# Attention followed by two quantized convolutions: products with v in half steps, and what moves with them

## The chip, the cores and the metric

The kernel runs on one core of a Trainium2 chip. The metric is the time of one execution on the device in microseconds (us); lower is better. A profiled execution gives its own time, and a span from its first to its last instruction.

## What is computed

An input x of 4 images, 128 channels, 64 x 64 positions goes through a group norm, an attention over the 4096 positions with four heads of 32 channels, a projection and a residual sum. The result goes through two 3 x 3 convolutions with weights quantized to 3 bits, each followed by a batch norm; the first has a relu, the second adds its input and then has a relu. The reference, cut:

```python
x_norm = _group_norm(x, norm_w, norm_b)
qkv = jnp.einsum('oc,bchw->bohw', qkv_w, x_norm) + qkv_b[None, :, None, None]
...
attn = jnp.einsum('bhid,bhjd->bhij', q, k) * scale
attn = jax.nn.softmax(attn, axis=-1)
out = jnp.einsum('bhij,bhjd->bhid', attn, v)
...
out = jnp.einsum('oc,bchw->bohw', proj_w, out) + proj_b[None, :, None, None]
x = x + out
...
residual = x
out = conv3x3_decomposed(x, lsq_quantize(w1, alpha1))
out = jax.nn.relu(batchnorm(out, gamma1, beta1))
out = conv3x3_decomposed(out, lsq_quantize(w2, alpha2))
out = batchnorm(out, gamma2, beta2)
out = jax.nn.relu(out + residual)
```

`lsq_quantize` divides the weights by a step, clips, rounds and multiplies back.

## The kernel before

**Blocks and steps.** The attention is cut into 32 blocks, eight blocks of 512 queries (`qb`) for each of four images (`b`), and each block into 32 steps (`kt`) of 128 keys. A step has two score pairs and the products with v. `scores` computes one pair, that is two heads: eight TensorE matmuls of 512 columns into a PSUM tile `s` of two banks (three such tiles rotate), and one ScalarE exponential of 128 x 1024 (L437) into half of a tile `p`. The `p` tiles come from `ppool`, which has eight buffers. `weights` does the products of a step: for each of the four heads a matmul of 128 x 32 weights from v with 512 columns of `p`, which the profile shows as two records, all added into one bank `acc` over the block (L448). The four heads use four column tiles of the array side by side; four matmul records that run together are called a group below. The scores use two row tiles.

**Sums.** The softmax's denominator is the sum of all `p` of a block. VectorE adds 26 of the 32 tiles (L458, L460); the steps in `MOVED` are added by DMAs that POOL issues (L453, L455), and `merge` (L481) joins the two. The matmuls of `total` (L477) sum over partitions.

**The order on TensorE** is written out by hand: three pairs, one step of products, three pairs, two steps of products, and so on. Scores run ahead of products. Side work is put at places given by steps: `schedule(n, before)` returns a list of (step, function), and after each step of products `side` runs what is due. `slots` are the steps whose number in the whole run is divisible by 3, which are those done singly; the matmuls of side work go there. Side work of a block is: the end of the block before (`sums`, `spread`, `invert`, `gather`, `weigh`, `project`, `store`), the projections to q, k and v of the next image's chunks of 512 positions (`project_parts`, in `visit`, with the copy of the result one step later: for k and q L344 on ScalarE and L345 on VectorE, for v L364 on VectorE), group norm statistics, and loads. For image 0 the chunks are projected in blocks 0 and 1 from two `p` tiles that hold x (`xh`).

**Quantization.** `quant_tasks` yields pieces: for each of the two convolutions nine scalar operations, and three times three taps, each with a load (L172) and thirteen VectorE operations (L174 to L189) into the resident tiles `wq[0]` and `wq[1]`. The pieces are taken up six to a block, in blocks of the last image from its second on.

**Convolutions.** Images are cut into bands of 16 rows. A band is loaded (`load_band`, issued by SP), split into two parts of fewer bits (`split_band`, VectorE, L562 and L563), and each half band takes 18 matmuls of 512 columns (L752). The first two bands are loaded and split in the last attention block; the third is loaded after `sums_at_once` and split after the last `store`. The later ones follow in `first(m)`. After that `att.close()` gives the attention's memory to the convolution's tiles (`mid`). At the end each of 16 pieces is scaled and added (L912, VectorE), goes through a relu (L913, ScalarE) and leaves by a DMA issued by SP (L914).

Queues work in order: an instruction that waits holds up what stands behind it on its engine, DMA issues on SP, POOL and ACT among them.

Of the kernel before, what the change touches and what calls it, by code (L numbers as in the profile page):

```python
# [16 lines left out]
F32 = mybir.dt.float32  # L17
# [5 lines left out]
P = 128  # L23
GROUP = 16
HEADS = 4
D = 32
# [52 lines left out]
def _fast_body(ctx, tc, x, norm_w, norm_b, qkv_wt, qkv_b, proj_wt, proj_b,  # L79
# [57 lines left out]
    wq = [const.tile([P, TAPS, P], F32R, name=f"wq{i}") for i in range(2)]  # L137
# [3 lines left out]
    def quant_tasks(pool):  # L141

        tasks = []
        for i, (w, alpha) in enumerate(((w1, alpha1), (w2, alpha2))):
# [20 lines left out]
            for c in range(3):  # L165


                def taps(i=i, c=c, w=w, t=t):
                    tk, tq = (pool.tile([P, 2, FB], F32, name=f"t{n}{i}{c}", tag=n) for n in "kq")
                    wr, q0, qh, ql = (u[:, e, : 3 * P].rearrange("p (t o) -> p t o", o=P)  # L170
                                      for u in (tk, tq) for e in range(2))
# [17 lines left out]
                    nc.vector.tensor_scalar(wq[i][:, 3 * c : 3 * c + 3, :], q0, ROUND, None,  # L189
                                            ALU.subtract)  # L190
# [9 lines left out]
    dram = ctx.enter_context(tc.tile_pool(name="dram", bufs=1, space=bass.MemoryType.DRAM))  # L200
# [11 lines left out]
    ppool = att.enter_context(tc.tile_pool(name="ppool", bufs=8))  # L212
# [228 lines left out]
    def weights(step):  # L441
# [3 lines left out]
        if kt == 0:  # L445
            acc[n] = psa.tile([P, FB], F32, name=f"acc{n}", tag="a")
        for h in range(HEADS):
            nc.tensor.matmul(acc[n][h * D : (h + 1) * D, :], v[:, kt % KB, h * D : (h + 1) * D],  # L448
                             pt[:, h, :], start=(kt == 0), stop=(kt == NK - 1))
# [172 lines left out]
    def schedule(n, before):  # L622
        b, qb = blocks[n]
        todo = []
        slots = [kt for kt in range(NK - 1) if (n * NK + kt) % 3 == 0]
        two = b + 1 < B and qb in (2, 3)
        full = two or n == 1

        def add(kt, f):
            todo.append((kt, f))  # L630

        def visit(kts, first, second, evacuate=None):
            add(kts[0], first)
            add(kts[-1], second)
            if evacuate:
                add(kts[-1] + 1, evacuate)

        if before:
            add(1, before["merge"])
            kts = slots[3:4] if full else slots[3:5]  # L640
            visit(kts, lambda: before["sums"](0), lambda: before["sums"](1))
            kt = kts[-1]
            add(kt + 1, before["spread"])
            add(kt + 3, before["invert"])
            add(kt + 4, before["gather"])
            add(kt + 6, before["residual"])
            add(slots[9] - 2, before["weigh"])
            add(slots[9], before["project"])
            add(slots[9] + 1, before["store"])
        if n + 1 < len(blocks):  # L650
            add(22 if n == 0 else 14, lambda: load_q(*blocks[n + 1]))
        if n == 0:
            for kt, what, j in ((0, "k", 4), (3, "k", 5), (6, "v", 4), (9, "k", 6), (12, "v", 5),
                                (15, "k", 7), (18, "q", 1), (21, "v", 6), (24, "v", 7)):
                visit((kt,), *first_chunk(j, what, False))
                if what == "k":
                    add(kt + 2, lambda j=j: load_k(0, j))
        if n == 1:
            for i, j in zip((0, 1, 2, 4, 5, 6), range(2, NB)):
                visit(slots[i : i + 1], *first_chunk(j, "q", False))  # L660
        if b + 1 < B:
            if qb == 1:
# [6 lines left out]
                for i in (0, 1):  # L669
                    add(slots[7 + i], late[b][1 + 2 * i])  # L670
                    add(slots[7 + i] + 1, late[b][2 + 2 * i])
            if qb == 2:
                add(slots[0], late[b][5])
                add(slots[0] + 1, late[b][6])
                add(slots[0] + 1, late[b][7])
                add(slots[0] + 2, late[b][8])
            chunks = {1: (), 2: (0, 1), 3: (2, 3), 4: (4,), 5: (5,), 6: (6,), 7: (7,)}
            for i, j in enumerate(chunks.get(qb, ())):
                p = project_parts(b + 1, j, lambda j=j: xin[b + 1, j])
                if not two:  # L680
                    places = dict(k=slots[0:2], q=slots[5:7], v=slots[7:9])
# [692 lines left out]
```

## Time and profile before

| what | us |
|---|---|
| runs before: median of 3 (lowest, highest) | 2571.59 (2570.69, 2572.87) |
| profiled execution, its own time | 2571.87 |
| its span | 2570.1 |
| attention, from the first pair to the last product | 25 to 2256 |
| first convolution, to its last matmul | 2256 to 2398 |
| second convolution, to its last matmul | 2402 to 2540 |
| scaling and output | 2540 to 2570 |

The granted TensorE clock is 0.994 of the full one on average. In lines of the timeline the columns are: start, length, engine, source line, operation, tiles and shapes, number of instructions merged into the line, and in brackets how long the engine idled before and what ended that. The length of a matmul line reaches past the start of the next one, since matmuls are pipelined and their ends are modelled; the distance between starts is what TensorE takes. In a table of windows the columns are the stretch, its length, the busy time (and number) of PE, PEld, DVE, ACT and POOL, then the clock, the share of the 16 DMA engines, and GB/s. In a group of the page: busy time, mean ns of one, and the idle time before with its releaser.

### The profile page before, as it was taken

How to read it: one execution, taken by the hardware profiler on the slowest of the kernel's cores; microseconds unless marked ns; L12 is line 12 of the kernel's file. 1: busy time of each engine (PE TensorE's matmuls, PEld its weight loads, DVE VectorE, ACT ScalarE, POOL GpSimd, SP SyncE). 2: the span in 40 equal slices, each digit the busy share in tenths (PEclk: the TensorE clock that was granted, in tenths of full speed). 3: DMA queues.
4: the chain of work that ended last, by engine and by line, in shares of the span. 5: the costliest groups of instructions: out<-in, count | busy, mean ns of one | idle time of the engine just before them, and what ended most of it. 6: DMA issues, size and time to landing. Idle time of an engine off the chain costs nothing.

```text
span 2570.1 us, 48634 instructions
## 1 busy us (share of the span) xinstructions
PE 2526.5 (98%) x20504; PEld 1231.7 (48%) x20504; DVE 2139.0 (83%) x1401; ACT 2083.9 (81%) x2278; POOL 280.3 (11%) x459
## 2 busy tenths in 40 slices
PE   9999999999999999999999999999999999999995
PEld 5444444444444444444444444444444444467774
DVE  6898888888988889889988888888999998854345
ACT  5888899998989899998988899998889899911224
POOL 2111111111011111110011111110000001000000
PEclk9999999999999999999999999999999999999997
DMA  6777666788667767787766666986755756635004
GB/s 193 186 189 177 173 157 156 167 195 192 164 144 183 173 156 166 161 214 175 165 171 158 164 158 151 205 202 141 160 115 131 164 125 141 147 79 162 1 1 165
DMA packets 147562, 400.06 MB, mean 156 GB/s; under 512 B 59256, under 2 KB 60024, under 8 KB 118792
## 3 DMA queue, kind: packets, MB, share of 16 engines
q0 software_dynamic: 45792, 280.33, 48.4%
q1 hardware_dynamic: 100824, 115.10, 16.9%
q8 instruction: 163, 2.67, 0.4%
q10 hardware_dynamic: 720, 1.44, 0.2%
q14 instruction: 63, 0.52, 0.1%
HBM read 105.32 MB, written 55.83 MB: 63 GB/s over the span
## 4 chain that ended last, share of the span: by engine, by line
PE 82%; DVE 9%; DMA 4%; issue 3%; ACT 1%; SPq 0%; POOL 0%; DVEq 0%; POOLq 0%; ACTq 0%
PE s L435 36%; PE acc L448 32%; PE c L752 9%; DVE r L460 6%; DMA rm<-p 4%; PE l L477 1%; PE pk L310 1%; PE pq L310 1%; PE po L310 1%; PE pv L310 1%; ACT p L437 1%; DVE res L912 1%; PE c_last L752 0%; DMA xh<-in_x_dram 0%; DVE r L458 0%
## 5 line engine op out<-in xcount | busy, mean ns | idle before, releaser
L437 ACT ACTIVATE p<-s 128x1024 f32<-128x1024 f32 x2048 | 1940.3, 1032 | 229.3 <-PE s L435 153.8
L460 DVE TENSOR_TENSOR r<-r,p 128x2048 f32<-128x2048 f32 x768 | 1758.4, 2290 | 93.8 <-ACT p L437 45.1
L435 PE MATMUL s<-q,k 64*128 64x512 f32 x8192 | 1160.5, 412 | 3.1 <-ACT p L437 2.5
L448 PE MATMUL acc<-p,v 128*32 128x512 f32 x8192 | 1021.9, 601 | 0.5 <-DVE v L364 0.5
L435 PEld LDWEIGHTS s<-q,k 64*128 64x128 f32 x8192 | 709.1, 185 | 632.5 <-issue 296.1
L448 PEld LDWEIGHTS acc<-p,v 128*32 128x32 f32 x8192 | 197.8, 108 | 452.9 <-issue 446.1
L455 POOL DMA_DIRECT2D rm<-p x160 | 138.5, 866 | 946.4 <-ACT p L437 770.1
L817 ACT COPY cv<-c 128x512 f32<-128x512 f32 x60 | 35.3, 588 | 201.9 <-DVE st L816 201.9
L752 PE MATMUL c<-hi,wq 128*128 128x512 f32 x540 | 139.2, 402 | 2.8 <-DVE hi L562 1.6
L752 PE MATMUL c<-lo,wq 128*128 128x512 f32 x540 | 138.6, 401 | 0.0
L816 DVE BATCH_NORM_STATS2 st<-c 128x6 f32<-128x512 f32 x60 | 41.9, 699 | 104.3 <-PE c L752 84.1
L752 PEld LDWEIGHTS c<-hi,wq 128*128 128x128 f32 x540 | 101.2, 188 | 32.5 <-DVE hi L562 2.5
L752 PEld LDWEIGHTS c<-lo,wq 128*128 128x128 f32 x540 | 101.6, 188 | 27.1
L458 DVE TENSOR_TENSOR r<-p,p 128x2048 f32<-128x2048 f32 x32 | 73.3, 2290 | 23.9 <-ACT p L437 23.8
L345 DVE SCALAR_TENSOR_TENSOR kst<-pk,b,kst 128x512 fp32r<-128x512 f32 x32 | 24.0, 750 | 72.1 <-ACT kst L344 72.1
L345 DVE SCALAR_TENSOR_TENSOR qst<-pq,b,qst 128x512 fp32r<-128x512 f32 x32 | 24.0, 750 | 41.5 <-ACT qst L344 41.3
L481 POOL DMA_DIRECT2D r<-rm x31 | 26.3, 849 | 162.0 <-PE s L435 79.8
L453 POOL DMA_DIRECT2D rm<-p x32 | 17.8, 558 | 228.6 <-ACT p L437 142.9
L349 POOL DMA_DIRECT2D qd<-qst x31 | 23.1, 747 | 177.9 <-DVE qst L345 160.8
L349 POOL DMA_DIRECT2D kd<-kst x28 | 20.7, 738 | 167.5 <-DVE kst L345 164.1
L477 PE MATMUL l<-r,ones 128*32 128x256 f32 (+1 forms) x504 | 37.9, 383 | 0.5 <-issue 0.5
L310 PE MATMUL po<-av,wp 128*32 128x512 f32 x256 | 33.4, 594 | 4.2 <-DVE av L526 4.2
(146 smaller groups left out, 722.9 us busy)
## 6 DMA issues: line engine op xcount, KB each, us to landing
rm<-p POOLq DMA_DIRECT2D x192, 1024.0 KB, 7.9
q<-qd SPq DMA_DIRECT2D x248, 128.0 KB
r<-rm POOLq DMA_DIRECT2D x31, 1024.0 KB, 7.7
x<-in_x_dram SPq DMA_DIRECT2D x80, 256.0 KB
k<-kd SPq DMA_DIRECT2D x124, 128.0 KB
qd<-qst POOLq DMA_DIRECT2D x31, 512.0 KB, 5.9
kd<-kst POOLq DMA_DIRECT2D x28, 512.0 KB, 3.7
y<-x POOLq DMA_DIRECT2D x32, 256.0 KB, 4.8
```

The lines of the kernel that those rows point to most:

```text
L310: nc.tensor.matmul(out[cs, :], w[:, cs], x, start=True, stop=True)
L345: nc.vector.scalar_tensor_tensor(lo, ps[what], bias, t[:, 0, :], ALU.add, ALU.subtract)
L349: (nc.sync if start else nc.gpsimd).dma_start(out=dst[b, j].rearrange("s p n -> p s n"), in_=t)
L435: nc.tensor.matmul(s[:, i, :], k[r, half, c0 : c0 + P], q[r, half, part, :], start=(part == 0), stop=(part == 1))
L437: nc.scalar.activation(pts[step][:, 2 * half : 2 * half + 2, :], s, AF.Exp, scale=SCALE)
L448: nc.tensor.matmul(acc[n][h * D : (h + 1) * D, :], v[:, kt % KB, h * D : (h + 1) * D], pt[:, h, :], start=(kt == 0), stop=(kt == NK - 1))
L455: nc.gpsimd.dma_start(out=msum[n], in_=pt, accum_op=ALU.add)
L458: nc.vector.tensor_tensor(rsum[n], pts[step - 1], pt, ALU.add)
L460: nc.vector.tensor_tensor(rsum[n], rsum[n], pt, ALU.add)
L477: nc.tensor.matmul(t["l"][h * D : (h + 1) * D, cs], ones, r[:, h, cs], start=first, stop=end)
L752: nc.tensor.matmul(ps.rearrange("p (r w) -> p r w", w=W), w[:, tap, :], part[:, r0 + kh : r0 + kh + RB, kw : kw + W], start=(n == 0), stop ...
L816: nc.vector.bn_stats(st[:, b * NB + c, :], ps[:, j, :])
```

## The change

Seven things are changed together.

1. **Half steps.** `weights(step, half)` does 256 of the 512 columns of a step. The order is now three pairs and three half steps throughout; before the first, six pairs are done instead of five. Only the first matmul of the first half starts the accumulation, and only the last of the second half ends it. Sums and moved tiles follow the second half.
2. **Places in half steps.** `ends` are the last half steps of each round of three, 21 in a block where `slots` had 10 or 11. Side work is put there with `at_half`; `visit` takes the index of a place and does both halves there, or on it and the next with `split`. The copy of a projection follows one half step after its second half.
3. **Image 0.** Queries 2 to 7 of image 0 are projected from x that is loaded again, so that `xh` is free after block 0. Statistics and projections of image 1 start one block later, and three blocks instead of two take two chunks each.
4. **`ppool` has nine buffers.** The room comes from `wq[1]`.
5. **Quantization.** Three pieces a block in the last image's first seven blocks; six and five in the first blocks of the second and third image. The second convolution's weights go to DRAM (`wqd`) by DMAs of POOL, are loaded again after `att.close()` by SP, and are copied to `wq[1]` by VectorE in `first(6)`.
6. **Third band.** Loaded in the last block and split ahead of `sums_at_once`.
7. **Output.** Every other piece leaves by a DMA that ScalarE issues.

The diff, cut to its core:

```diff
-    wq = [const.tile([P, TAPS, P], F32R, name=f"wq{i}") for i in range(2)]
+    wq = [const.tile([P, TAPS, P], F32R, name="wq0")]
+    wqd = dram.tile([P, TAPS, P], F32, name="wqd")
...
+                    if i == 0:
+                        nc.vector.tensor_scalar(wq[0][:, cs, :], q0, ROUND, None, ALU.subtract)
+                    else:
+                        nc.vector.tensor_scalar(ql, q0, ROUND, None, ALU.subtract)
+                        nc.gpsimd.dma_start(out=wqd[:, cs, :], in_=ql)
+                    yield
...
-    ppool = att.enter_context(tc.tile_pool(name="ppool", bufs=8))
+    ppool = att.enter_context(tc.tile_pool(name="ppool", bufs=9))
...
-    def weights(step):
+    def weights(step, half):
...
+        cs = slice(half * FB // 2, (half + 1) * FB // 2)
         for h in range(HEADS):
-            nc.tensor.matmul(acc[n][h * D : (h + 1) * D, :], v[:, kt % KB, h * D : (h + 1) * D],
-                             pt[:, h, :], start=(kt == 0), stop=(kt == NK - 1))
+            nc.tensor.matmul(acc[n][h * D : (h + 1) * D, cs], v[:, kt % KB, h * D : (h + 1) * D],
+                             pt[:, h, cs], start=(kt == 0 and half == 0),
+                             stop=(kt == NK - 1 and half == 1))
+        if half == 0:
+            return
...
-        slots = [kt for kt in range(NK - 1) if (n * NK + kt) % 3 == 0]
-        two = b + 1 < B and qb in (2, 3)
+        ends = [p for p in range(2 * NK - 2) if (2 * n * NK + p) % 3 == 2]
+        two = b + 1 < B and qb in ((3, 4, 5) if b == 0 else (2, 3))
...
+        def visit(i, first, second, evacuate=None, split=True):
+            at_half(ends[i], first)
+            e = ends[i + 1 if split else i]
+            at_half(e, second)
             if evacuate:
-                add(kts[-1] + 1, evacuate)
+                at_half(e + 1, evacuate)
+            return e
...
+                    for what, i in dict(k=1, q=10, v=13).items():
+                        visit(i, *p[what])
+                    continue
+                for what, e in (dict(k=2, q=7, v=9) if i == 0 else dict(k=11, q=13, v=15)).items():
+                    visit(e, *p[what], split=False)
...
-        if b == B - 1 and 0 < qb < NB - 1:
-            for kt in range(1, NK - 1, 5):
+        if b == B - 1 and qb < NB - 1:
+            for kt in (1, 10, 20):
                 add(kt, lambda: next(pieces, None))
+        elif 0 < b and qb == 0:
+            for kt in (1, 10, 15, 20, 25) + ((29,) if b == 1 else ()):
+                add(kt, lambda: next(pieces))
...
+            add(27, lambda: load_band(0, 2))
...
-    run_scores(2)
-    while at["step"] < steps:
-        for s, w in ((3, 1), (3, 2)):
-            run_scores(s)
-            run_weights(w)
+    run_scores(3)
+    while at["half"] < 2 * steps:
+        run_scores(3)
+        run_weights(3)
...
     conv(ready[0, 0, 0], early[0][:, 1, :], 1, wq[0])
+    split_band(*bandlist[2])
     last["sums_at_once"]()
-    load_band(*bandlist[2])
...
     last["store"]()
-    split_band(*bandlist[2])
...
+    raw_w = mid.tile([P, TAPS, P], F32, name="raw_w")
+    wq.append(mid.tile([P, TAPS, P], F32R, name="wq1"))
+    nc.sync.dma_start(out=raw_w, in_=wqd)
...
+        if m == 6:
+            nc.vector.tensor_copy(wq[1], raw_w)
...
-                nc.sync.dma_start(out=out[b].rearrange("c h w -> c (h w)")[:, cs], in_=y)
+                eng = nc.sync if j % 2 == 0 else nc.scalar
+                eng.dma_start(out=out[b].rearrange("c h w -> c (h w)")[:, cs], in_=y)
```

## The prediction

> **What bounds the kernel now.** I read the page's busy times first, then its costliest groups.
>
> ```profile
> PE 2526.5 (98%) x20504; PEld 1231.7 (48%) x20504; DVE 2139.0 (83%) x1401; ACT 2083.9 (81%) x2278; POOL 280.3 (11%) x459
> ...
> L437 ACT ACTIVATE p<-s 128x1024 f32<-128x1024 f32 x2048 | 1940.3, 1032 | 229.3 <-PE s L435 153.8
> L460 DVE TENSOR_TENSOR r<-r,p 128x2048 f32<-128x2048 f32 x768 | 1758.4, 2290 | 93.8 <-ACT p L437 45.1
> L435 PE MATMUL s<-q,k 64*128 64x512 f32 x8192 | 1160.5, 412 | 3.1 <-ACT p L437 2.5
> L448 PE MATMUL acc<-p,v 128*32 128x512 f32 x8192 | 1021.9, 601 | 0.5 <-DVE v L364 0.5
> ```
>
> TensorE looks always busy, so only stretches that are longer than they need be can be won. To find them I went through the timeline of PE for the whole attention part (25 to 2256 us) and sorted its 682 rounds, a round being three score pairs and the products with v behind them. A stretch without side work, with ACT beside it:
>
> ```profile
> 1893.47 1.66 PE L435 MATMUL s<-q,k 64*128 64x512 f32 x12
> 1894.25 5.61 ACT L437 ACTIVATE p<-s 128x1024 f32<-128x1024 f32 x6 [0.60 <-PE s L435]
> 1895.06 1.06 PE L448 MATMUL acc<-p,v 128*32 128x512 f32 x8
> 1896.06 1.84 PE L435 MATMUL s<-q,k 64*128 64x512 f32 x12
> 1897.83 1.92 PE L448 MATMUL acc<-p,v 128*32 128x512 f32 x16
> ```
>
> From start to start: three pairs 1.59 us, one step of products 1.00, three pairs again but 1.77, two steps 1.85. The second group of pairs is the stretched one, and ACT then idles 0.60 us per two rounds. A round with side work:
>
> ```profile
> 1942.24 1.67 PE L435 MATMUL s<-q,k 64*128 64x512 f32 x12
> 1943.84 1.06 PE L448 MATMUL acc<-p,v 128*32 128x512 f32 x8
> 1944.73 0.61 PE L477 MATMUL l<-r,ones 128*32 128x256 f32 x8
> 1945.27 1.67 PE L435 MATMUL s<-q,k 64*128 64x512 f32 x12
> ```
>
> This round takes 3.03 us and the pairs after it start 1.60 us ahead of their products: nothing is stretched. Over all rounds the means are: pairs 1.595; one step of products 0.996, two steps 1.854; 0.432 more for eight side matmuls of 256 columns, 0.863 for sixteen, 0.857 for eight of 512. What exceeds these is the whole reserve, 37 us: 21.9 in pairs after the 117 short rounds (2.59 us, no side work; 0.19 each), 4.3 in a few other pairs that wait up to 1.2 us, mostly for a p buffer (ACT waits on the DMA rm<-p 4.5 us in all), 8.2 in product phases, 2.7 at the start. Where the products wait, VectorE is late:
>
> ```profile
> 1908.11 2.29 DVE L460 TENSOR_TENSOR r<-r,p 128x2048 f32<-128x2048 f32 x1
> 1910.31 0.68 DVE L526 TENSOR_TENSOR av<-av,rc 128x512 f32<-128x512 f32 x1
> ...
> 1911.05 1.07 PE L310 MATMUL po<-av,wp 128*32 128x512 f32 x8 [2.45 <-DVE av L526]
> ```
>
> That block (1846.74 to 1917.20) has VectorE busy 68.4 of 70.5 us. Last, the convolution's one hole and the end:
>
> ```profile
> 2277.70 2.42 PE L752 MATMUL c<-hi,wq 128*128 128x512 f32 x9 [1.56 <-DVE hi L562]
> ...
> 2556.00:2560.00 4.00, 0.00 (x0) 0.00 (x0) 4.00 (x4) 3.85 (x4) 0.00 (x0) 0.50 1.02 407
> ```
>
> The last columns of the window are clock, DMA share and GB/s: all 16 DMA engines are full while the output leaves.
>
> **What the Trainium skill says.** "TensorE: Matmul & The Clock Gate", section "Wait — 56ns, not 53.3ns?", gives a fixed cost of about 2.5 ns per matmul beside its columns. The trace agrees: two groups of 256 columns take 432 ns, one of 512 takes 429 (0.858/2). The same page's opening table says that TensorE's queue pulls weight loads ahead of running matmuls. The trace agrees: the four loads of a group (0.13 us) lie under the group before. "TensorEngine Tiling (Array Packing)", section "Key Properties": changing the tiling mode drains the engine. It fits 0.996 - 0.858 = 0.138 us once per product phase; the number of changes stays. "Trainium Kernel Development and Optimization", section "Key Constraints": DMAs issued by SP, ACT and POOL share the same 16 engines, and issuing from several saves issue time only. The share of 1.02 with one queue agrees.
>
> **The change part by part**, against the profiled execution, 2571.87 us (span 2570.1 and 1.8 around it; 0.3 above the median of the runs).
>
> *Equal phases.* Every round becomes three pairs and three half steps: 1.595 + 0.138 + 1.294 = 3.03 us. ACT needs 2.86 for three exponentials. In the quoted stretch ACT begins 0.78 us after the pairs do and has released the third bank at 0.78 + 2.86 = 3.64; a short round wants to write it at 2.59 + 1.07 = 3.66, which, with the release taking about 0.18, gives the measured 0.17 to 0.19. A 3.03 us round wants it at 4.10, so 0.28 remains. In the trace the 141 rounds near 3.03 us are followed by pairs with no excess beyond one-off waits. All 21.9 go: **-21.9**.
>
> *Halves.* Each step has four groups of 256 columns instead of two of 512: 2048 more groups at 2.4 ns, **+5.0** (683 phases x 0.0074). Their loads (16,384 instructions added, half of them loads) hide under groups of 216 ns, as those of pv hide under 109 ns groups.
>
> *ACT's other work.* Bias copies of k and q (L344, 0.70 us busy) are queued half a step after the visit, thus behind the next round's three exponentials. Before, that was a two-step round with 0.6 us of ACT idle; now it is a 3.03 us one with 0.17. The next exponential comes about 0.36 us late against 0.28 of cover: 0.1 us. There are 59 such copies, and where the round behind one carries a side product it costs nothing; with the copies of acc and l I take half of 6 us, **+3**. Bounds: 0, and the whole 0.36 x 59 = 21.
>
> *Nine p buffers.* The DMA rm<-p holds a tile 7.9 us in the median and 14.8 at most; a ninth buffer gives a step (2.1 us) more, above the longest single wait (1.4): -3.3 of the 4.3, since other small waits may sit there (bounds 0 and -4.3). Dropping xh after block 0 frees two more in block 1.
>
> *Quantization.* Three taps cost 13 VectorE operations, 6.2 us by their rows, 37 in all. Before, six pieces per block put about 9 us into each of blocks 25 to 28; now three pieces are 3.7 us in blocks 24 to 30, and 6 to 8 in blocks 8 and 16, which have no projections. The waits of po on av (4.2 us) and the stretched pairs behind the longest (0.8) go: **-5.0**. Block 8 is followed by a block with bn_stats (8 x 0.69 us), where VectorE has little left: **+1**, bounds 0 and 4. The second weights' three stores on POOL and the single reload are 1.2 MB of 400 and cost nothing. POOL waits for ql before each store; behind it stands an rm<-p with one buffer more of slack.
>
> *Third band.* Its split moves into the 7 us in which VectorE is idle ahead of L499: -1.6. But the reload of the second weights stands on SP ahead of the fourth band's load and goes to memory that the attention's tiles held; the memset of L807, to the same region, waited until 2279.9 for VectorE. If the load waits as long, the band lands about 5 us later, near 2285, when TensorE (from 2276.1, 8.6 us on) wants it: +1, bounds 0 and +3. Together **-0.6**. The copy to wq1 (some 0.8 us of VectorE) lies in one of the 4.4 us gaps ahead of L816.
>
> *Output on two queues.* Sixteen half-megabytes at 405 GB/s are 21 us, from 2545 to 2566.3; a second queue adds no engine. ACT now issues eight of them (SP's take 0.33 us each): two activations and an issue are about 2.6 us against 2.6 for two transfers. **0**, bounds -0.8 (the one gap near 2546) and +2.
>
> Sum: -21.9 + 5.0 + 3 - 3.3 - 5.0 + 1 - 0.6 = -21.8, so 2550.1, and **2550** beside the median. Start (2.7), sums, projections, load rates and the convolutions stay. What is late next is TensorE itself: 2.02 us a step with nothing left to squeeze.
>
> **Rivals.**
> 1. *Bias copies cost their whole shift.* For it: ACT's idle time per round falls from 0.6/2 to 0.17. Against: the slack of 0.28. Time: 2550 + 18 = 2568. Chance 0.10.
> 2. *Half groups don't stream* (slower). In the product phases of 24 matmuls and 24 loads, a group takes 0.226 us instead of 0.216, because a load of 0.13 us is not always finished, or 1.8 times the product instructions don't arrive in time. 4096 groups x 0.010 = 41: 2591. It decides from 22/4096, some 5 ns a group. For it: so long a run of half groups is nowhere in the trace. Against: 16 side matmuls of 256 follow eight of 512 at 0.216, and 32 of 128 columns at 0.109. Chance 0.09.
> 3. *No residue*: no late ACT, all p waits gone, the whole 1.6 at the band: 2550 - 3 - 1 - 1 - 1 - further product waits of 3 = 2541. Chance 0.07.
> 4. Forecast: 0.74, its own range 2542 to 2561.
>
> **How the numbers follow.** About 0.2% (5 us) is what this kernel's measurement tells from no change. Faster, below 2566.4: forecast, no residue and a third of the first rival, 0.84. Within: the rest of that rival, 0.07. Slower: 0.09. The range 2540 to 2569 takes in the first rival and leaves out the slow one and the far ends, under 0.2 together.
>
> **What would show it.** Pairs at 1.60 us in nearly every round and rounds of 3.03; product phases of 1.43 with 24 matmuls; no po wait on av near 1900; the hole at 2277.70 gone or below 1.5 us; the end still at 400 GB/s. Groups of 256 above 0.22 us, or pairs above 1.65 us in the second round after bias copies, would make it wrong.

## The result, and the profile after

| | before | after |
|---|---|---|
| median of 6 runs each, us | 2573.67 | 2566.55 |
| ratio of after to before (95% interval) | | 0.9976 (0.9963 to 0.9989) |
| the profiled execution, us | 2571.87 | 2569.21 |
| its span | 2570.1 | 2567.4 |
| first pair | 25.2 | 28.5 |
| attention, first pair to the copy of the last acc | 2231.2 | 2222.9 |
| from there to the end of the span | 313.7 | 316.0 |

The kernel got faster by 0.24%, 7 us in the medians. The forecast was 21.8 us. The two profiles differ by 2.7 us only, because the profiled execution of the changed kernel began its attention 3.3 us later. That is not the change: the kernel before with one edit inside the attention (b_halves, below) begins at 28.7 us too. The start goes with TensorE's granted clock ahead of the first pair. In the profile of the kernel before the clock does not fall back there; in five of the variants below it falls to half for 3.4 us, and they begin between 26.8 and 27.6; in the changed kernel and the seven others it does so for 6.8 us, and they begin between 28.1 and 29.4. So attention and the rest are compared stage by stage here, and whole times by their medians.

The page of the changed kernel, first the busy times and then its costliest groups (busy time, mean ns of one, idle time before them and its main releaser):

```profile
PE 2515.2 (98%) x28696; PEld 1504.3 (59%) x28696; DVE 2137.1 (83%) x1402; ACT 2086.7 (81%) x2278; POOL 282.9 (11%) x462
...
L444 ACT ACTIVATE p<-s 128x1024 f32<-128x1024 f32 x2048 | 1949.6, 1032 | 216.0 <-PE s L442 161.4
L471 DVE TENSOR_TENSOR r<-r,p 128x2048 f32<-128x2048 f32 x768 | 1758.2, 2289 | 69.4 <-ACT p L444 18.7
L442 PE MATMUL s<-q,k 64*128 64x512 f32 x8192 | 1140.6, 409 | 6.7 <-ACT p L444 5.5
L456 PE MATMUL acc<-p,v 128*32 128x256 f32 x16384 | 1027.1, 383 | 1.0 <-DVE v L371 1.0
```

The scores (L442, L435 before) lost 20 us of busy time, the products (L456, L448 before) with twice the matmuls gained 5. This is what the change was made of, and it is close to the forecast. The last field of the scores' row has grown: 5.5 us in which TensorE waited for an exponential, against 2.5 before. The lines of TensorE and ScalarE in the timeline of a stretch without side work:

```profile
1930.62 1.50 PE L456 MATMUL acc<-p,v 128*32 128x256 f32 x24
1932.06 1.64 PE L442 MATMUL s<-q,k 64*128 64x512 f32 x12
1932.83 5.85 ACT L444 ACTIVATE p<-s 128x1024 f32<-128x1024 f32 x6 [0.17 <-PE s L442]
1933.63 1.50 PE L456 MATMUL acc<-p,v 128*32 128x256 f32 x24
1935.06 1.65 PE L442 MATMUL s<-q,k 64*128 64x512 f32 x12
```

From start to start: pairs 1.57 us, products 1.43, again and again. ACT idles 0.17 us per round instead of 0.60 per two. Over the whole attention, 665 of 682 rounds have pairs between 1.56 and 1.62 us, 1.595 in the median, and product phases without side work take 1.43. In the steady state the forecast (1.595 and 1.432) came out to the hundredth. So the question is where the rest of the gain went. The view of waits, for TensorE and the attention's window alone (total us, times, longest):

```profile
PE s L442 <- ACT p L444: 5.5, 10, 3.1
PE pq L317 <- DMA x<-in_x_dram: 2.9, 2, 2.7
PE pq L317 <- ACT av L481: 1.1, 1, 1.1
PE pk L317 <- DVE bvn L296: 1.0, 1, 1.0
PE acc L456 <- DVE v L371: 1.0, 1, 1.0
```

A few single waits, none of them in the steady state. Three places hold most of them.

*The second block.* From the timeline, SP's own queue (SPq) and the one matmul that waits:

```profile
139.33 0.58 SPq L534 DMA_DIRECT2D rc<-rd  x1
...
140.05 1.71 SPq L235 DMA_DIRECT2D x<-in_x_dram  x3
...
141.87 8.41 SPq L422 DMA_DIRECT2D q<-qd  x8
...
146.84 1.07 PE L317 MATMUL pq<-x,wn 128*32 128x256 f32 x16 [2.67 <-DMA x<-in_x_dram]
...
150.46 0.35 SPq L235 DMA_DIRECT2D x<-in_x_dram  x1
```

For image 0 the queries' chunks are now projected from x fetched anew. The fetches stand on SP behind `gather` (rc), which waits for the reciprocals' way through DRAM, and the last one also behind eight loads of q. TensorE stands still for 2.67 us. With smaller waits for the copy of acc (1.06 us) and for `merge` (0.75) this block takes 76.6 us; before it took 73.2.

*The seams between images.* Block 23 ends at 1716.6 us. The timeline there, without the matmuls and additions that go on as always:

```profile
1715.32 3.52 SPq L411 DMA_DIRECT2D k<-kd  x4
1715.49 0.84 POOL L466 DMA_DIRECT2D rm<-p  x1 [2.79 <-DMA rm<-p]
...
1718.95 0.37 SPq L415 DMA_DIRECT2D v<-vd  x1
1719.37 0.46 SPq L175 DMA_DIRECT2D tk<-in_L_conv_w_dram  x1
...
1727.88 4.69 ACT L444 ACTIVATE p<-s 128x1024 f32<-128x1024 f32 x5 [3.96 <-DMA rm<-p]
1728.06 0.83 POOL L492 DMA_DIRECT2D r<-rm  x1 [11.73 <-DMA rm<-p]
```

The DMA that adds step 28's `p` to rm was issued at 1715.49 and let POOL go on at 1728.06, 12.6 us later; over the run the accumulating ones (L466) take 7.9 us from issue to landing in the median. Beside it run the loads of the next image's keys and values and a load of weights for quantization. In these 12.6 us SP's queue moves 1.54 MB, beside the 1.05 MB that the DMA reads. ACT waits 3.96 us for that `p` buffer, and TensorE with it; for the 3.4 us from 1729.15 on, the granted clock is at half besides. The same seam in the kernel before:

```profile
1702.41 6.39 SPq L404 DMA_DIRECT2D k<-kd  x4
...
1707.74 0.83 POOL L455 DMA_DIRECT2D rm<-p  x1 [2.68 <-DMA rm<-p]
...
1716.75 5.61 ACT L437 ACTIVATE p<-s 128x1024 f32<-128x1024 f32 x6 [0.79 <-DMA rm<-p]
```

There step 28's DMA had 0.76 MB of SP's beside it, and ACT waited 0.79 us. At the other two seams of the changed kernel the waits are smaller: 0.83 and 1.75 us (593.5, 614.5) and 2.28 us (1162.9). The one at 1162.9 is for step 24's DMA, which takes 11.8 us there with 1.44 MB of SP's beside it; step 28's was issued only after it.

*The way to the convolution.* From the timeline, SP, VectorE and TensorE:

```profile
2274.79 0.33 SPq L808 DMA_DIRECT2D raw_w<-wqd  x1
...
2275.18 17.25 SPq L582 DMA_DIRECT2D t<-y  x6
...
2281.59 0.78 DVE L573 CAST hi<-t 128x1188 fp32r<-128x1188 f32 x1 [4.80 <-DMA t<-y]
...
2282.52 3.71 PE L781 MATMUL c<-hi,wq 128*128 128x512 f32 x9 [2.51 <-DVE hi L573]
```

The old hole at 2277.70 is gone, since the third band is split in time. A new one of 2.51 us follows for the fourth band: its load could be issued only behind the reload of the second weights, at 2275. Before, SP had issued that load, and the next, by 2253 us. After the hole nine matmuls take 3.71 us instead of 2.3.

### The profile page after: what moved, and what is told of

It reads as the page before. It is cut to its first block, busy times and chain, and to the rows that moved or that the text cites. A ratio compares the mean times of both kernels' runs of the same rounds, so it can differ in the third digit from the quotient of the medians.

```text
span 2567.4 us, 65010 instructions
## 1 busy us (share of the span) xinstructions
PE 2515.2 (98%) x28696; PEld 1504.3 (59%) x28696; DVE 2137.1 (83%) x1402; ACT 2086.7 (81%) x2278; POOL 282.9 (11%) x462
## 4 chain that ended last, share of the span: by engine, by line
PE 85%; DMA 6%; issue 4%; DVE 3%; ACT 1%; SPq 0%; POOL 0%; ACTq 0%; POOLq 0%; DVEq 0%
PE s L442 38%; PE acc L456 34%; PE c L781 8%; DMA rm<-p 3%; DVE r L471 2%; PE pk L317 1%; PE l L488 1%; PE po L317 1%; PE pq L317 1%; PE pv L317 1%; DMA t<-y 1%; ACT p L444 1%; DMA rd<-rq 0%; ACT res L946 0%; DMA x<-in_x_dram 0%
## 5 line engine op out<-in xcount | busy, mean ns | idle before, releaser
L442 PE MATMUL s<-q,k 64*128 64x512 f32 x8192 | 1140.6, 409 | 6.7 <-ACT p L444 5.5
L456 PE MATMUL acc<-p,v 128*32 128x256 f32 x16384 | 1027.1, 383 | 1.0 <-DVE v L371 1.0
L442 PEld LDWEIGHTS s<-q,k 64*128 64x128 f32 x8192 | 715.1, 185 | 417.4 <-issue 167.7
L456 PEld LDWEIGHTS acc<-p,v 128*32 128x32 f32 x16384 | 462.6, 109 | 485.6 <-issue 249.2
L466 POOL DMA_DIRECT2D rm<-p x160 | 139.1, 870 | 848.0 <-ACT p L444 602.7
L352 DVE SCALAR_TENSOR_TENSOR kst<-pk,b,kst 128x512 fp32r<-128x512 f32 x32 | 24.0, 750 | 81.3 <-PE s L442 54.9
L469 DVE TENSOR_TENSOR r<-p,p 128x2048 f32<-128x2048 f32 x32 | 73.2, 2288 | 14.9 <-ACT p L444 14.9
L351 ACT ACTIVATE kst<-pk,b 128x512 fp32r<-128x512 f32 x32 | 22.3, 700 | 18.4 <-PE pk L317 18.4
L317 PE MATMUL pq<-x,wn 128*32 128x256 f32 x480 | 33.3, 379 | 3.9 <-DMA x<-in_x_dram 2.9
```

What stands on the lines that cost most here:

```text
L317: nc.tensor.matmul(out[cs, :], w[:, cs], x, start=True, stop=True)
L352: nc.vector.scalar_tensor_tensor(lo, ps[what], bias, t[:, 0, :], ALU.add, ALU.subtract)
L442: nc.tensor.matmul(s[:, i, :], k[r, half, c0 : c0 + P], q[r, half, part, :], start=(part == 0), stop=(part == 1))
L456: nc.tensor.matmul(acc[n][h * D : (h + 1) * D, cs], v[:, kt % KB, h * D : (h + 1) * D], pt[:, h, cs], start=(kt == 0 and half == 0), stop= ...
L466: nc.gpsimd.dma_start(out=msum[n], in_=pt, accum_op=ALU.add)
L469: nc.vector.tensor_tensor(rsum[n], pts[step - 1], pt, ALU.add)
```

## The experiments

Kernels called a_ are the changed kernel with an edit, b_ is the kernel before with one. All ratios are to the kernel before, measured on the same chip beside them. Differences in us between two variants are differences of medians that were not taken beside each other, some of them on different chips. The changed kernel's own (2566.55) and that of a_one_queue below, which turns out to be the same (2568.52; both have the ratio 0.9976), show how far two such medians can lie apart: about 2 us. Blocks of the traces carry the verdicts on single places. A block in which nothing waits mostly repeats within 0.1 us. One with a wait does not, so for these the spread over the traces is given.

**1. Equal phases undone (a_unequal).**

```diff
-    run_scores(3)
-    run_weights(3)
+    for w in (2, 4):
+        run_scores(3)
+        run_weights(w)
```

`ends` follows, with the half steps that end these phases; one VectorE step goes two half steps earlier, as the order needs it.

> The changed kernel with everything kept (halves, nine buffers, quantization places, third band, two queues) except that the product phases take 2 and 4 halves in turn instead of 3 and 3; the side work keeps its numbers and goes to the ends of these phases. Theory A (equal phases are worth what the prediction said; the gain was lost in single waits elsewhere): the 21.9 us come back, about 2588 us against 2566.5, ratio to before about 1.006, and the pairs behind the short phase show 1.6 to 1.7 us instead of 1.59. Theory B (the equal phases themselves bring less than priced): under 2578 us, ratio under 1.002.

Measured: 2604.17 us, ratio 1.0118 (1.0103 to 1.0134). The lines of TensorE and ScalarE in the same stretch as above:

```profile
1933.19 5.61 ACT L444 ACTIVATE p<-s 128x1024 f32<-128x1024 f32 x6 [0.44 <-PE s L442]
1934.01 1.07 PE L456 MATMUL acc<-p,v 128*32 128x256 f32 x16
1935.01 1.82 PE L442 MATMUL s<-q,k 64*128 64x512 f32 x12
1936.77 1.93 PE L456 MATMUL acc<-p,v 128*32 128x256 f32 x32
```

Pairs behind a short phase start 1.76 us ahead of their products, as in the kernel before. The product phases cost the same as two equal ones (1.00 + 1.86 against 2 x 1.43), so all of the loss is in the pairs. It is 37.6 us in the medians and 38.9 in the attention, more than the 21.9 forecast. The kernel before put its side work into the short rounds and so had only 117 bare ones; here some 230 rounds are short and bare, at about 0.17 us each. Theory A holds, B falls: pairs behind bare short rounds cost what the prediction said, and this kernel has twice as many of them. The undoing itself thus shows the cost of one, and not the 21.9; those follow from the 117 in the kernel before.

**2. Halves alone (b_halves).** The kernel before, each product as two halves of 256 columns:

```diff
+        for half in range(2):
+            cs = slice(half * FB // 2, (half + 1) * FB // 2)
             for h in range(HEADS):
-                nc.tensor.matmul(acc[n][h * D : (h + 1) * D, :], ..., pt[:, h, :], ...)
+                nc.tensor.matmul(acc[n][h * D : (h + 1) * D, cs], ..., pt[:, h, cs], ...)
```

> The kernel before with one edit: each product with v is issued as two halves of 256 columns one after the other (twice the matmuls and weight loads), in the old phases of one and two steps. Theory A (halves stream as full matmuls do and cost their starts alone, 5.0 us in the prediction): 2577 to 2579 us against 2573.3, ratio 1.001 to 1.002; the short phase stays near 1.00 and the long near 1.86 us. Theory F (halves cost much more, and this is where the gain went): 10 us or more, ratio above 1.004.

Measured: 2577.8 us, ratio 1.0016 (1.0008 to 1.0025), so 2 to 6 us, 3.8 in the medians. The attention grew by 4.9 (2236.1), of which 2.8 lie in the second block, with a wait of 1.74 us and half the clock for 3.4 us behind it. The steadier measure is the phases: bare short ones grew from 0.996 to 1.001 us in the median and long ones from 1.854 to 1.864, two and four more groups at 2.4 ns, as priced. Theory A; the term of 5.0 was right.

**3. Second block (a_block1).**

```diff
-            for i, j in zip((0, 2, 8, 10, 12, 14), range(2, NB)):
+            for i, j, e in zip((1, 3, 8, 10, 12, 14), range(2, NB), (0, 0, 2, 4, 8, 10)):
                 if j > 3:
-                    at_half(ends[i - 3], lambda j=j: fetch(0, j))
+                    at_half(ends[e] + 1, lambda j=j: fetch(0, j))
```

with the sums at the sixth end instead of the fifth and the next q loaded at step 19 instead of 14.

> The changed kernel, in its second block alone: the input chunks of the query projections are fetched earlier (chunk 4 at the third end of a phase, 5 at the fifth, 6 at the ninth, 7 at the eleventh), the first two projections go one phase later, the sums go one phase later, and the next queries are loaded at step 19 instead of 14. Theory A (TensorE waits in order behind SP's queue for the fetched chunk): the waits for x (2.67 and 0.4 us), for the copy of acc (1.06) and for the merge (0.95) go, that block falls from 76.6 to 71 or 72 us, and the time by 4 to 6 us: about 2561 us, ratio 0.995. Theory D (the block is bound by the exponentials and by two product banks anyway): block above 75 us, time 2565 to 2568.

Measured: 2560.88 us, ratio 0.9955 (0.9941 to 0.9968). The block takes 71.01 us instead of 76.57; all other blocks but those at the seams, the first and the last are as they were. In the six traces without this edit and with equal phases the block takes 75.6 to 79.2 us, in all five with it 71.0. Theory A.

**4. The reload of the second weights later (a_reload_late).**

```diff
-    nc.sync.dma_start(out=raw_w, in_=wqd)
...
             load_band(*bandlist[m + 3])
+        if m == 3:
+            nc.sync.dma_start(out=raw_w, in_=wqd)
```

> The changed kernel, with the reload of the second convolution's weights from DRAM moved on SP's queue from ahead of the fourth band's load to behind the seventh band's. Theory A (the reload waits for the attention's memory and holds the band loads behind it): the 2.5 us hole of TensorE near 2282 us and the low clock behind it go, 4 to 5 us less from the last attention work to the end (316.7 to about 312), about 2562 us, ratio 0.9955. Theory E (the band's load waits for the stores of y0 or for memory of its own): the hole stays, 2565 to 2568.

Measured: 2564.65 us, ratio 0.9968 (0.9956 to 0.998). From the last copy of acc to the end: 312.0 us instead of 316.0 (the 316.7 in the expectation is counted from the last product). The fourth band's split and its first matmuls in this kernel:

```profile
2271.85 0.76 DVE L573 CAST hi<-t 128x1188 fp32r<-128x1188 f32 x1
2272.65 1.40 DVE L574 TENSOR_TENSOR lo<-t,hi 128x1188 fp32r<-128x1188 f32 x1
...
2274.99 2.31 PE L781 MATMUL c<-hi,wq 128*128 128x512 f32 x9
```

No wait is left, and nine matmuls take 2.31 us throughout. Theory A holds, E falls. The total moved by 2 us only, which is inside what two medians can differ by; the stage shows 2 to 4.5: 314.2 to 316.6 us in the seven traces of the changed kernel and its variants without this edit, 311.7 to 312.4 in the five with it.

**5. Keys and values later in the program (a_kv_later).** Chunks 5 and 6 are loaded at steps 3 and 7 of the next image's first block, chunk 7 at step 12.

> The changed kernel, with the loads of keys and values of the next image's chunks 5 and 6 moved out of the last block of an image into its first block (steps 3, 7, and chunk 7 at step 12). Theory A (exponentials stand still at the seams between images, since the added-up exponentials' DMA shares the DMA engines with these loads and frees its p buffer late): the waits of ScalarE for the DMA rm<-p at about 605, 1160 and 1726 us go, and with them 7 to 9 us: about 2558 us, ratio 0.994. Theory C (the chain of accumulating DMAs is slow by itself): the waits stay, 2564 to 2569 us.

Measured: 2566.63 us, ratio 0.9971 (0.996 to 0.9983): a miss. Block 15 fell from 73.00 to 71.05, block 24 stayed at 73.26. But at block 24 this was no test of theory A: SP still issued chunks 5 and 6 at 1703.4 and 1708.1 us, ahead of the block's end at about 1714 and hardly later than before the edit (1704.7 and 1709.0, with the end at 1716.6). Only chunk 7 moved, from 1715.3 to 1744.9. A place in the program sets the order on SP's queue, not the time; SP runs ahead until something it needs is missing. That the waiting is done by the issuing engine, and not by the DMA engines, is what the Trainium skill says too ("DMA: Bandwidth & Descriptors", section "Anatomy of one DMA — SWDGE (gpsimd) path": "DMA engines do not wait on semaphores"). The trace agrees: chunk 7, placed behind SP's next wait for the sums, left at 1744.9, 0.65 us after that wait ended, while chunks 5 and 6 had no such wait left ahead of them.

**6. Eight buffers (a_p8).** `ppool` with `bufs=8`.

> The changed kernel with eight buffers of exponentials instead of nine. Prediction: 3.3 us (0 to 4.3) come back, 2570 us, ratio 0.999. Theory A of the seams (the DMA rm<-p frees its buffer late while keys and values are loaded, and six pairs of lead leave less room than five did): the waits of ScalarE for rm<-p at the three seams grow by about one step each, 2 us or more apiece, and new ones appear: 6 to 10 us in all, ratio 1.000 to 1.002. Theory G (buffers don't matter): ratio 0.997 to 0.998.

Measured: 2577.27 us, ratio 1.0013 (1.0006 to 1.0019), so 9 to 11 us come back instead of 3.3. ACT's waits for the DMA rm<-p between 500 and 2200 us are 17.9 us in ten places, the longest 5.0; with nine buffers they are 8.8 in four. Theory A of the seams, whose 6 to 10 us are nearly met; the forecast of 3.3 is missed.

**7. Quantization put back (a_quant_back).**

```diff
-        if b == B - 1 and qb < NB - 1:
-            for kt in (1, 10, 20):
+        if b == B - 1 and 0 < qb < NB - 1:
+            for kt in range(1, NK - 1, 5):
                 add(kt, lambda: next(pieces, None))
-        elif 0 < b and qb == 0:
-            for kt in (1, 10, 15, 20, 25) + ((29,) if b == 1 else ()):
-                add(kt, lambda: next(pieces))
```

> The changed kernel with the quantization pieces back in six blocks of the last image, at steps 1, 6, 11, 16, 21 and 26 of each. Prediction: 4 to 5 us come back, blocks 25 to 30 grow by 0.7 us or so each (65.25 and 68.30 now), the seam at 1726 us gets no weight load beside it and may shrink: 2568 to 2571 us, ratio 0.9985. Theory H (with equal phases VectorE has room, so the places don't matter): 2565 to 2567, ratio 0.997.

Measured: 2573.88 us, ratio 0.9997 (0.9989 to 1.0004), 5 to 7 us more. The size is as forecast, the shape is not: blocks 25 to 28 grow by 0.7 in all, and block 29 by 7.55, by one wait. From its timeline:

```profile
2091.61 8.63 SPq L422 DMA_DIRECT2D q<-qd  x8
...
2100.88 0.50 SPq L175 DMA_DIRECT2D tk<-in_L_conv_w_dram  x1
...
2108.52 0.42 DVE L177 TENSOR_SCALAR tk<-tk,inv 128x384 f32<-128x384 f32 x1 [6.43 <-DMA tk<-in_L_conv_w_dram]
...
2114.25 0.69 DVE L537 TENSOR_TENSOR av<-av,rc 128x512 f32<-128x512 f32 x1
...
2114.99 1.94 PE L317 MATMUL po<-av,wp 128*32 128x512 f32 x8 [5.71 <-DVE av L537]
```

VectorE itself waited 6.43 us for a load of weights, and the sums and `weigh` stood behind that. The load and its first use are two pieces, here 5 steps apart instead of 9 to 13. That alone does not make the wait: the kernel before has the same 5 steps, its six loads were issued 9.3 to 49 us ahead of their use, and none was waited for; of the six here, five had 19 to 52 us. The sixth stood on SP behind eight loads of q, left at 2100.88, and had 7.6. So the 5 to 7 us are mostly one late load, and not the room on VectorE that the prediction had in mind: the other blocks show 0.7 us for that, and the other waits of po on av come to 1.0 us in all. That the size was met is luck. The place on SP is read from one trace; it was not varied.

**8. Three places mended (a_three).** Edits 3 and 4, chunks 0 to 2 at steps 1, 5, 9, 3 and 4 at 20 and 26, 5 to 7 at 3, 7, 12 of the next block, and the VectorE step of edit 1.

> The changed kernel with the second block's fetches (as in a_block1) and the reload of the second weights (as in a_reload_late) moved, the loads of the next image's keys and values placed away from SP's wait for the sums (chunks 0 to 2 at steps 1, 5, 9, chunks 3 and 4 at 20 and 26 of the last block, 5 to 7 at 3, 7, 12 of the next), and one small VectorE step two half steps earlier. Theory A (the gain was lost in these single waits): the waits for rm<-p at 605, 1160 and 1726 us shrink to under 1 us each, second block 71, last attention work to end 312, in all 14 to 18 us less than the changed kernel: 2549 to 2552 us, ratio 0.991. Theory C (the accumulating DMAs are slow by themselves): the seams stay and 2556 us is left, ratio 0.9935.

Measured: 2555.06 us, ratio 0.9926 (0.9913 to 0.9939). Block 1 and the end are as forecast (71.01; 312.4), the seams are not (block 24: 73.07). Theory C seemed to gain, but SP had again run ahead: two batches of loads left at 1701 and 1707 us, with the block's end at about 1708.

**9. The loads tied to a later event (a_pool_kv).** As a_three, but chunks 5 and 6 are issued by POOL, which at that place waits for the merge anyway, and chunks 3 and 4 come on SP behind its wait for the gathered reciprocals. Against the changed kernel:

```diff
-                for j in range(NB - 1):
-                    add(4 * j + 1, lambda j=j: load_kv(b + 1, j))
+                for j, kt in ((0, 1), (1, 5), (2, 9), (3, 18), (4, 19)):
+                    add(kt, lambda j=j: load_kv(b + 1, j))
         if b > 0 and qb == 0:
-            add(1, lambda: load_kv(b, NB - 1))
+            for j, kt, eng in ((5, 2, nc.gpsimd), (6, 5, nc.gpsimd), (7, 12, nc.sync)):
+                add(kt, lambda j=j, eng=eng: load_kv(b, j, eng))
```

> As a_three, but the loads of the next image's chunks 5 and 6 are issued by GpSimd's queue behind the merge of the finished block's sums (SP, which has no work of its own to wait for, had run ahead of the program and issued them in the last block all the same), chunks 3 and 4 on SP behind its wait for the gathered reciprocals, chunk 7 on SP at step 12. Theory A (the seam waits come from DMA engines filled by these loads while the last rm<-p runs): the last rm<-p of blocks 7, 15 and 23 lands in 8 us or less instead of 11 to 14, the waits of 1 to 4 us at the seams go, block 24 falls from 73.1 to 67 or below, 2546 to 2549 us, ratio 0.9895. Theory C (the accumulating DMAs are slow by themselves): the waits stay and the time is 2553 to 2557.

Measured: 2548.93 us, ratio 0.9901 (0.9886 to 0.9916). The same seam, lines of POOL and ACT:

```profile
1704.89 0.84 POOL L466 DMA_DIRECT2D rm<-p  x1 [2.37 <-ACT p L444]
...
1712.33 0.83 POOL L492 DMA_DIRECT2D r<-rm  x1 [6.60 <-DMA rm<-p]
1712.72 2.86 ACT L444 ACTIVATE p<-s 128x1024 f32<-128x1024 f32 x3 [0.17 <-PE s L442]
1713.08 2.29 POOL L411 DMA_DIRECT2D k<-kd  x4
```

The last rm<-p takes 7.4 us instead of 12.6 (12.3 in a_three), the loads follow it, and ACT waits for nothing but TensorE. Block 24 falls from 73.07 to 68.28, which is what the blocks 27 and 30 take. SP's queue moves 0.02 MB beside it instead of 1.54. At the second seam step 24's DMA takes 8.1 us instead of 11.8, and block 15 falls to 70.96. At these two seams theory A holds and C falls: the accumulating DMA was slow because it shared the engines. The first seam is different. There SP's loads were small beside the last rm<-p already in the changed kernel (0.30 MB), it takes 9.7 us with them and without, and the wait of 1.75 us behind it is 1.46 here; what makes it stays open. Two more waits in block 8, of 0.82 and 1.83 us, come behind POOL's new loads, which hold up the rm<-p that follow them.

**10. The other end of the same wait (a_no28).** As a_three with the loads where the changed kernel has them, but step 28 of blocks 7, 15 and 23 is added by VectorE:

```diff
-        if kt in MOVED:
+        if kt in (MOVED[:-1] if n in (7, 15, 23) else MOVED):
```

> As a_three but with the loads of keys and values where the changed kernel has them; instead, in blocks 7, 15 and 23 step 28's exponentials are added by VectorE and not by the accumulating DMA (2.35 us more of VectorE in each). Theory A (the buffer that step 28's DMA holds is what ScalarE waits for): the seam waits go, 2547 to 2552 us. Theory I (VectorE, near its bound in these blocks, then frees the buffers late in its turn): waits of 1 us or more on VectorE's r appear at the seams, 2553 to 2558 us.

Measured: 2550.62 us, ratio 0.9905 (0.989 to 0.992). Block 24 is 68.28 here too, with the loads untouched: what ACT waited for there is the buffer that step 28's DMA holds. Theory I falls; no wait on VectorE's r appears. At the second seam a wait of 1.51 us for a DMA rm<-p stays, and block 15 takes 72.24 us against 70.96 in a_pool_kv, as fits a wait for step 24's DMA.

**11. Output on one queue (a_one_queue).** `eng = nc.sync` in the last loop.

> The changed kernel with the output's DMAs on SP's queue alone. Prediction: no difference (between 2 us faster and 1 us slower), ratio 0.997 to 0.998; the last stretch from the end of the last convolution to the end of the span is the same within 0.5 us.

Measured: 2568.52 us, ratio 0.9976 (0.9969 to 0.9984), the changed kernel's own. From the start of the last nine matmuls of the convolutions to the end of the span: 32.5 us in both, and in the kernel before.

**12. The better way at each seam (a_best).** a_no28's at the first, a_pool_kv's at the others.

> As a_pool_kv at the second and third seam between images, as a_no28 at the first (loads of keys and values where the changed kernel has them, step 28 of block 7 added by VectorE). Theory A (each seam's wait is independent of the others, so the better of the two ways can be taken at each): blocks 7 and 8 together 133.8 us instead of 135.6, the others as in a_pool_kv, 2547 us, ratio 0.9895. Against it: the blocks' gains are not kept side by side, 2549 to 2551.

Measured: 2550.59 us, ratio 0.9911 (0.9897 to 0.9925); not told apart from a_pool_kv, and not the 2547 of theory A. Blocks 7 and 8 together are 134.2 us instead of 135.6, the others are kept; its profiled execution lost that by its start (first pair at 28.9 instead of 27.5, first block 81.5 instead of 80.5).

Where the time is, in us, from one profiled execution each:

| | before | after | a_three | a_pool_kv | a_no28 |
|---|---|---|---|---|---|
| block 0 | 78.6 | 80.7 | 80.9 | 80.5 | 81.3 |
| block 1 | 73.2 | 76.6 | 71.0 | 71.0 | 71.0 |
| blocks 7, 8, 15, 24 | 275.9 | 281.8 | 280.8 | 274.8 | 274.4 |
| all blocks | 2231.2 | 2222.9 | 2214.9 | 2207.9 | 2208.8 |
| from there to the end | 313.7 | 316.0 | 312.4 | 311.7 | 312.2 |

## Why the prediction was wrong

*What bounds the kernel: right.* Stretched pairs behind short rounds were the reserve, and it was won. The measured time lies next to the 2568 us of the first rival, but that is chance: pairs behind the copies of q take 1.59 us in the median, and of the 28 behind copies of k five take 1.66 to 1.70, some 0.4 us in all. Half groups stream.

*Equal phases, -21.9: right,* by the rounds of the trace, and by their undoing as the cost of one stretched pair.

*Halves, +5.0: right* (2 to 6). *Bias copies, +3: too much,* at 0.4. *Output, 0: right*, for the reason given, with 32.5 us either way.

*Nine p buffers, -3.3: this step failed, and with it the sign.* The bounds went from -4.3 to 0. The prediction took the waits for rm<-p from the old kernel and let one more buffer cover them. In the changed kernel they are 8.8 us instead of 4.5, and the four blocks at the seams take 5.9 us more than before. The ninth buffer is needed (without it 9 to 11 us more), but it does not suffice: the last rm<-p of an image lasts up to 12.6 us when SP's loads share the 16 DMA engines with it. In the old kernel the longest took 14.8 us, with waits of 1.4 at most, so it matters where a long one falls. What moved them against each other was in no step of the prediction. In the old kernel three of the seven chunks loaded in block 23 left SP ahead of its wait for the sums, in the changed one only two, so a batch more came behind it: the last one began 7.3 us ahead of the block's end before (1702.4 of 1709.7), 1.2 us ahead after (1715.3 of 1716.6). Scores also run six pairs ahead of the products in every round, instead of five and six in turn. How much each of the two adds is open. The last batch is not all of it: in a_kv_later it begins 5.9 us ahead of the end, and ACT still waits 3.57 us. Nor is it the load of weights at 1719.37: in a_quant_back the weights are loaded elsewhere, and block 24 takes 73.3 us all the same. That moving the loads, or taking step 28 from the DMA, ends the wait at block 24 was shown (a_pool_kv, a_no28).

*"Start (2.7), sums, projections, load rates and the convolutions stay": failed in block 1.* The prediction counted the gain of dropping xh and not the fetches that replace it, with their place on SP behind `gather`. It lost 3.4 us against the old kernel there, and 5.6 against what the block can take (a_block1). In block 0 about 2 us were lost: its first pairs take 5.8 us to the first product instead of 4.3, with six pairs instead of five and a wait for q of 1.0 us instead of 0.4, and a product waits 1.0 us for v instead of 0.5. These two were read, not tried.

*Third band, -0.6: the mechanism was named, and mis-sized.* The hole of 1.6 us went, and the reload on SP held up the fourth band as described, but at a cost of 4 us in this trace, not 1 (316.0 against 312.0): 2.5 of waiting, and the rest at the lower clock that followed. The prediction's bound was 3; over the traces the cost is 2 to 4.5.

*Quantization, -5.0 + 1: right in size* (5 to 7), by luck: the undoing lost most of it to one late load. The waits of po on av that the prediction listed (4.2 us before, 0.9 after) stay near 1 us, but for that one load, when the pieces go back.

The sum of the mis-sized terms, against the forecast of -21.8: p buffers and seams 9.2 (5.9 instead of -3.3), block 1 3.4 more than before, block 0 2.2, end 2.9 (2.3 instead of -0.6), bias copies -2.6: 15.1, where the medians are 14.7 short. That these agree so well is more than the terms can carry: each is from one trace, block 1 alone varies by 3 us between traces, and the seams' blocks also hold a share of the other terms. With block 1, the seams and the end mended (a_pool_kv) the time is 25.4 us below the kernel before beside it, 3.6 more than forecast.

## What to carry to other kernels

Where an engine is busy almost all the time, price the steady state from its rounds, and then walk through every place where the change alters the order on a DMA queue: here the steady state gave all it promised, and two thirds of the gain were lost again, most of it in the second block, at the seams and on the way to the convolution. A DMA's place in the program is an order on its queue and not a time; to keep a load away from another, tie it to an event that its queue waits for, such as POOL's merge. And a buffer that a DMA reads is held as long as the DMA lasts under the load of that moment: 12.6 us at the seam, not the median of 7.9.

## What the hardware showed

TensorE's clock fell to half after some single waits and not after others of the same length or longer. In the windows of the traces (length, busy times, then the granted clock, DMA share, GB/s), first the changed kernel behind its hole of 2.51 us at 2280:

```profile
2280.00:2282.00 2.00, 0.01 (x1) 0.00 (x0) 0.41 (x1) 0.00 (x0) 0.00 (x0) 1.00 1.41 218
2282.00:2284.00 2.00, 1.48 (x4) 1.22 (x5) 1.97 (x3) 0.00 (x0) 0.00 (x0) 0.53 1.40 218
2284.00:2286.00 2.00, 2.00 (x7) 1.61 (x6) 1.29 (x3) 0.73 (x2) 0.00 (x0) 0.62 1.40 217
2286.00:2288.00 2.00, 2.00 (x10) 1.54 (x10) 1.97 (x3) 0.44 (x1) 0.00 (x0) 1.00 1.36 223
```

Then the same kernel behind its hole of 2.67 us in block 1:

```profile
146.00:148.00 2.00, 1.17 (x18) 0.66 (x20) 1.55 (x1) 0.00 (x0) 0.00 (x0) 1.00 1.15 172
148.00:150.00 2.00, 2.00 (x24) 1.29 (x28) 0.00 (x0) 1.39 (x2) 0.00 (x0) 1.00 1.05 280
```

Last, a_p8 behind a hole of 1.52 us at 597.6:

```profile
600.00:602.00 2.00, 2.00 (x20) 0.87 (x16) 1.13 (x1) 1.23 (x2) 0.00 (x0) 0.50 1.08 230
```

The first hole costs more than 1 us on top (nine matmuls 3.71 us instead of 2.31), the second nothing. In a_kv_later even a hole of 3.26 us in block 1 leaves the clock at 1.00. Wherever a spell of half the clock follows a hole in the attention or the convolutions, in any of the traces, it lasts 3.4 or 6.8 us. This is one reason why blocks with a wait spread so much between executions, and a hole read from a single trace gives a poor price. The Trainium skill ("TensorE: Matmul & The Clock Gate", section "Part 1: The HAM clock gate") says that the clock is at half after at least one idle window of about 3.4 us, and that the windows run freely, whenever a kernel starts. The spells of 3.4 and 6.8 us fit such a window; that an idle stretch has to fill one does not fit, since holes of 1.52 and 2.51 us were enough here.

An accumulating DMA of 1 MB within SBUF (L466) took between 6.9 and 14.3 us from issue to landing in the changed kernel, with a median of 7.9. At the third seam it took 7.4 us with 0.02 MB of other loads beside it (a_pool_kv) and 12.6 us with 1.54 MB (the changed kernel).
